# Rearranging VectorE's work at three places of a conditioned transformer block kernel in float32

## The chip, the cores and the metric

The kernel runs on one core of a Trainium2 chip. The metric is the device time of one execution in microseconds; times of several runs are given as their median.

In profiles PE is TensorE (its weight loads PEld), DVE VectorE, ACT ScalarE, POOL GpSimd and SP SyncE, which issues most DMAs.

## The reference

Two batch entries of 2048 rows with 512 columns go through one block; everything is float32.

```
emb  = silu(cond) @ ada_w + ada_b                     # per entry, six rows of 512
shift_msa, scale_msa, gate_msa, shift_mlp, scale_mlp, gate_mlp = split(emb, 6)
norm  = ln(x) * (1 + scale_msa) + shift_msa
h     = gelu(norm @ ssm_w1 + ssm_b1)                  # exact gelu, 512 -> 512
x     = x + gate_msa * (h @ ssm_w2 + ssm_b2)          # 512 -> 512
norm2 = ln(x) * (1 + scale_mlp) + shift_mlp
hf    = gelu_tanh(norm2 @ ff_w1 + ff_b1)              # 512 -> 1024
out   = x + gate_mlp * (hf @ ff_w2 + ff_b2)           # 1024 -> 512
```

## The kernel before, in words

The 4096 rows are cut into eight blocks `i` = 0 to 7 of 512 rows; blocks 0 to 3 are of the first batch entry, 4 to 7 of the second. A block passes through four products, which the tiles are named for: `hA` (ssm first), `oA` (ssm second, added to x), `hC` (ff first) and `oC` (ff second, added to x). In steady state the order on TensorE is `hC_i`, `oA_(i+1)`, `oC_i`, `hA_(i+2)`.

No product is computed plainly. `hA`, `oA`, and block 0's `hC` and `oC` use seven half-size products, P1, P2, P6, P5, P7, P3, P4 in this order, in place of eight. Sums of quarters of both operands are made ahead, and the results of several products are collected in three PSUM banks, `y` (P1, P6, P7, P4), `x` (P2) and `v` (P5, P3). `hC` of blocks 1 to 7 is a list of 26 products (`HK_P`, counted from 0 here) over registers: the quarters of norm2 and sixteen `forms`, which the 20 steps of `HK_B` make from them (line 819). `oC` of these blocks (`residual_in_leaves`) runs P1, P5, P6 and P7 as whole products and splits the other three once more into "leaves", seven small products `r` = 0 to 6 in the same order, with P7's matmuls spread between them.

The schedule is written by hand: every engine executes its instructions in the order in which the program issues them. `hook(hooks, places, ops)` spreads a list of operations over named places, and a place's operations are issued when its product and the reading of its bank have been issued (for `hC` the places are the product numbers). A place may hold work for any engine, so a hook fixes the place in that engine's queue alone. A PSUM bank that a later product adds to, or that a later tile takes over, is free only when the reading has ended: that is what TensorE can wait for.

What the diff touches:

- `hidden` makes a first product. Its `after` reads the banks: `take_first` (line 639 on VectorE, 637 on ScalarE) copies P1, P6 and P5 out with the bias added, lines 645, 652 and 655 add P2, P7 and P3 to these copies on VectorE, and ScalarE applies the gelu. `on_act` says who does `take_first`. It is used for block 0's `hC` (two groups of half the columns each) and for `hA`.
- `gb5_0` (line 1061) multiplies the ff bias row by the gate of the first entry and subtracts one half from the other, `apart_row`. `seed` later copies that row into the banks of `oC_0`.
- A gate is folded into the second weights once per batch entry. At the end of block 3's iteration `weight_of_second` gives eight multiplications of `fw2` by the gate (VectorE, line 395) and four sums of it (GpSimd, line 347), and `leaves_of_weight` four sums for the double leaves and four for the single ones (VectorE, line 347). Their list `fold` is spread over `First(5)`, that is `hA_5`, then `hC_4` and `oA_5`.
- A norm is `stats` (VectorE), `scales` (GpSimd), `normal` (ScalarE, line 539, or VectorE), `turn` (VectorE transposes of 32 by 32, line 550), `move` (16 DMAs, line 559, which put the blocks in place) and `moved` (modulation by scale and shift, line 582 on ScalarE, 584 on VectorE). Then come the sums or forms.
- In `oC_i` line 735 reads whole products, lines 773 and 776 the leaves. P7's bank is read in two steps behind leaf `r` = 4.
- For block 7 there is no `hA` between `oC_6` and `hC_7`. Its 20 forms, `late_forms`, are made on VectorE while `oC_6` ends and `hC_7` begins: seven in `oC_6`, thirteen at products 0 to 4.

Of the kernel before, what the change touches and what calls it, by code (L numbers as in the profile page):

```python
# [140 lines left out]
def kernel(  # L141
# [16 lines left out]
    nc = tc.nc  # L158
# [459 lines left out]
    def hidden(name, rhs, wops, bT, func, lo, hi, g, hooks, order=ORDER, on_act=False):  # L618
# [14 lines left out]
        def take_first(dst, src, r):  # L633
            if on_act:
                for j in range(2):
                    b = bT[:, r * half + m0 + j : r * half + m0 + j + 1]
                    nc.scalar.activation(dst[:, j], src[:, j], AF.Identity, bias=b)
            else:
                nc.vector.tensor_tensor(dst, src, bias(r), ALU.add)  # L639

        def after(p, ps, _):
            if p == "P1":
                take_first(s1, ps["y"], 0)
# [3 lines left out]
            elif p == "P6":  # L647
                take_first(u2, ps["y"], 0)
            elif p == "P5":
                take_first(s5, ps["v"], 1)  # L650
# [57 lines left out]
    def residual_in_leaves(name, i, hops, wops, leaf_wops, kdim, hooks, last=False):  # L708
# [58 lines left out]
        places = {1: "P5", 3: "P7", 4: "R4", 5: "P3", 6: "P4"}  # L767
        for r, f in enumerate(LEAVES):
# [8 lines left out]
            if r == 4:  # L777
                read("P7", "22", "21")
# [44 lines left out]
    class First:  # L823


        def __init__(self, i, rhs, hooks, order=ORDER, hA=None, on_act=False):
            if hA is None:
                hA = big_tile(f"hA_{i}")
            self.i, self.lo, self.hi = i, hA[:, : KD // 2, :], hA[:, KD // 2 :, :]
            hidden(f"hA_{i}", rhs, w1_ops, b1T, AF.Gelu, self.lo, self.hi, 0, hooks, order, on_act)  # L830
# [10 lines left out]
    class Second:  # L841
# [6 lines left out]
        def group(self, g, rhs, hooks):  # L848
            hidden(f"hC_{self.i}_{g}", rhs, fw1_ops, fb1T, AF.Gelu_apprx_tanh, self.lo, self.hi, g, hooks)
# [210 lines left out]
    def gb5_0():  # L1060
        nc.vector.tensor_tensor(gb[5], gate[5, 0], gb[5], ALU.mult)
        apart_row(gb[5], nc.gpsimd)
# [31 lines left out]
    hook(hooks, ("P7",), [gb5_0] + n2_sums[1:] + [lambda c=c: n1[2].normal(c) for c in range(C)])  # L1094
# [9 lines left out]
    hook(hooks, ("P2",), [n1[2].move])  # L1104
# [4 lines left out]
    hC.group(0, n2[0].ops, hooks)  # L1109
# [34 lines left out]
    hA[2] = First(2, n1[2].ops, hooks, on_act=True)  # L1144
# [14 lines left out]
    for i in range(1, NBLK):  # L1159
# [5 lines left out]
        if i == 1:  # L1165
            leaf_wops, leaf_fold = leaves_of_weight(fw2_sb, fw2_s, nc.gpsimd)
            hook(hooks, (5, 7, 9, 11, 13, 14, 15, 16), leaf_fold)
# [12 lines left out]
        if fold:  # L1180
            hook(hooks, (0, 0, 1, 1), fold[:4])
            hook(hooks, (5,), fold[4:8])
        hook(hooks, (0, 0, 0, 0, 1, 1, 1, 2, 2, 3, 3, 4, 4), late_forms)
# [13 lines left out]
        if nxt:  # L1197
# [3 lines left out]
            if fold:  # L1201
                hook(hooks, ("P1", "P2", "P6", "P5", "P5", "P7", "P7", "P3"), fold[8:])
# [7 lines left out]
        fold = None  # L1210
# [5 lines left out]
        if nxt:  # L1216
# [3 lines left out]
            turns = ("P2", "P2", "P6") if nx2 else ("P1",)  # L1220
# [12 lines left out]
        if nxt:  # L1233
            moved = n2[i + 1].moved((None,) if nx2 else (None, nc.vector))
            hook(hooks, ("P7",) if nx2 else ("P5", "P7", "P5", "P7"), moved)
# [7 lines left out]
        if nxt:  # L1243
            late = {}

            def form(eng):

                fb[i + 1] = n2[i + 1].registers()
                return sums_of_registers(HK_B, fb[i + 1], (eng,))

            if not nx2:

                def late_form(n):
                    if n == 0:
                        late["ops"] = form(nc.vector)
# [3 lines left out]
                hook(hooks, ("R4",) * 3 + ("P3",) * 2 + ("P4",) * 2, late_forms[:7])  # L1259
                late_forms = late_forms[7:]  # L1260

        residual_in_leaves(f"oC_{i}", i, hC, fw2_ops, leaf_wops, KH // 2, hooks, last)
# [4 lines left out]
        if nx2:  # L1267
            run(form(nc.gpsimd))

        if refold5:  # L1270
            take_gate(5, b)
            fw2_ops, fold = weight_of_second(fw2_sb, fw2_s, gate[5, b], (nc.vector,))
            leaf_wops, leaf_fold = leaves_of_weight(fw2_sb, fw2_s, nc.vector)
            fold += leaf_fold
        hooks = {}
        if refold5:
            hook(hooks, ("P6",), [multiply_5])
            hook(hooks, ("P5", "P7", "P3", "P4"), fold[:4])
            fold = fold[4:]
# [51 lines left out]
```

## The time and the profile before

| | us |
|---|---|
| median of 3 runs | 597.12 (597.0 to 598.76) |
| profiled execution | 597.23 |
| its span, first to last instruction | 595.4 |
| PE busy | 582.9 (98%) |
| DVE busy | 405.9 (68%) |
| POOL busy | 388.8 (65%) |
| ACT busy | 234.3 (39%) |
| mean granted TensorE clock | 0.998 |

A row of a timeline gives the start in us, the time in us (of several instructions from the first's start to the last's end), engine, line, operation, what it writes and reads, the shapes and the number of instructions; in brackets the idle time of the engine before it and what ended it. A row of waits names the engine that waited, its line, what it waited for, and the total, the number and the longest of the waits. A row of a stretch gives its bounds and length, the busy time and the number of instructions of each engine, the granted clock, and the share and rate of the DMAs.

### The profile page before, as it was taken

To read this page: it belongs to the slowest core of one execution; us is meant where nothing else is said; L and a number is where in the kernel's file an instruction comes from. 1 tells how busy PE (TensorE), PEld (TensorE's weight loads), DVE (VectorE), ACT (ScalarE), POOL (GpSimd) and SP (SyncE) were. 2 spreads that over 40 slices of the span, in tenths; PEclk is the share of its full clock that TensorE was granted. 3 is DMA by queue.
4 is the path that set the end of the run, shared out by engine and by line. 5 is a ranking of instruction groups with operands and counts; after the bars stand their busy time and mean duration, and the time that the engine had idled before them with its cause. 6 is when DMAs were issued, how large, how long until landed. Compare 5 with 4: busy or idle time off the path is not lost.

```text
span 595.4 us, 8969 instructions
## 1 busy us (share of the span) xinstructions
PE 582.9 (98%) x3127; PEld 512.5 (86%) x3127; DVE 405.9 (68%) x734; ACT 234.3 (39%) x396; POOL 388.8 (65%) x471
## 2 busy tenths in 40 slices
PE   7999999999999999999999999999999999998997
PEld 4888888888889888998889988888888988897886
DVE  4978898897566475675756778864756446559663
ACT  2235437405532374134811456134553236121420
POOL 1875439999991968539983699938687293800260
PEclk9999999999999999999999999999999999999999
DMA  8990332300324105440153602231030400031002
GB/s 317 395 381 13 81 72 78 101 36 35 69 75 120 41 0 116 141 134 2 31 129 72 212 1 55 87 72 71 1 72 1 142 2 1 1 72 70 2 0 72
DMA packets 24376, 50.17 MB, mean 84 GB/s; under 512 B 4576, under 2 KB 5644, under 8 KB 23436
## 3 DMA queue, kind: packets, MB, share of 16 engines
q1 hardware_dynamic: 20608, 44.86, 24.1%
q10 hardware_dynamic: 3724, 4.75, 3.3%
q8 instruction: 25, 0.41, 0.3%
q14 instruction: 19, 0.16, 0.1%
HBM read 26.51 MB, written 8.40 MB: 59 GB/s over the span
## 4 chain that ended last, share of the span: by engine, by line
PE 85%; DVE 4%; POOL 4%; DMA 2%; issue 2%; SPq 1%; ACT 1%; DVEq 0%; POOLq 0%
PE py_oC L724 11%; PE px_hC L881 9%; PE py_hA L465 9%; PE py_hC L881 7%; PE pv_hC L881 7%; PE py_oA L465 7%; PE pl_oC_P_y L757 6%; PE pv_hA L465 4%; PE pv_oA L465 3%; PE pv_oC L724 3%; PE pl_oC_P_v L757 3%; PE px_hA L465 2%; PE py_oC L465 2%; PE py_hC L465 2%; PE px_oA L465 2%
## 5 line engine op out<-in xcount | busy, mean ns | idle before, releaser
L582 ACT ACTIVATE nT<-nT,mod,mod 128x512 f32<-128x512 f32 x54 | 39.6, 802 | 103.5 <-DMA nT<-blocks 78.0
L539 ACT ACTIVATE nT<-x,nmr,rstd 128x512 f32<-128x512 f32 x56 | 42.4, 803 | 53.6 <-POOL nmr L526 38.8
L347 POOL TENSOR_TENSOR hSC<-hClo,hChi 128x512 f32<-128x512 f32 (+1 forms) x17 | 20.6, 1216 | 61.4 <-ACT hChi L876 47.6
L724 PE MATMUL py_oC<-fw,hClo 128*128 128x256 f32 x224 | 54.2, 380 | 1.2 <-DVE x L735 1.2
L508 POOL TENSOR_SCALAR ve<-mv 128x4 f32<-128x4 f32 x16 | 3.7, 231 | 77.0 <-DVE mv L500 70.2
L499 DVE BATCH_NORM_STATS2 st<-x 128x6 f32<-128x512 f32 x64 | 43.4, 678 | 5.2 <-DMA x<-in_x_dram 4.9
L724 PEld LDWEIGHTS py_oC<-fw,hClo 128*128 128x128 f32 x224 | 40.4, 190 | 5.7 <-DVE x L735 1.4
L881 PE MATMUL py_hC<-forms,fw 128*128 128x256 f32 x168 | 40.8, 379 | 0.0
L550 DVE STREAM_TRANSPOSE blocks<-nT 128x512 f32<-128x512 f32 x56 | 37.8, 694 | 3.8 <-ACT nT L539 3.5
L898 DVE TENSOR_TENSOR hClo<-hClo,py_hC 128x512 f32<-128x512 f32 x42 | 28.4, 680 | 16.6 <-ACT hClo L895 10.2
L819 POOL TENSOR_TENSOR forms<-forms 128x256 f32<-128x256 f32 x48 | 35.6, 742 | 2.8
L881 PEld LDWEIGHTS py_hC<-forms,fw 128*128 128x128 f32 x168 | 31.8, 190 | 4.4
L687 DVE TENSOR_TENSOR x<-py_oA,x 128x512 f32<-128x512 f32 x32 | 22.0, 688 | 19.5 <-PE py_oA L465 14.3
L898 DVE TENSOR_TENSOR hChi<-hChi,pv_hC 128x512 f32<-128x512 f32 x35 | 23.3, 683 | 14.7 <-PE pv_hC L881 14.7
L465 PE MATMUL py_hA<-nT,w 128*128 128x256 f32 x128 | 30.4, 381 | 0.0
L881 PE MATMUL px_hC<-forms,fw 128*128 128x256 f32 x112 | 27.8, 380 | 0.5 <-DVE forms L819 0.5
L876 ACT ACTIVATE hClo<-hClo,colsT 128x256 f32<-128x256 f32 x56 | 25.3, 499 | 6.7 <-DVE hClo L898 6.2
L465 PE MATMUL py_oA<-w,hA 128*128 128x256 f32 x112 | 26.5, 379 | 0.0
L465 PEld LDWEIGHTS py_hA<-nT,w 128*128 128x128 f32 x128 | 23.7, 190 | 3.1 <-DVE hA L639 0.2
L819 POOL TENSOR_TENSOR forms<-nT,forms 128x256 f32<-128x256 f32 x36 | 25.8, 739 | 0.5
L876 ACT ACTIVATE hChi<-hChi,colsT 128x256 f32<-128x256 f32 x56 | 25.1, 496 | 1.9 <-DVE hChi L898 1.9
L895 ACT ACTIVATE hClo<-px_hC 128x512 f32<-128x512 f32 x21 | 12.5, 597 | 33.7 <-PE px_hC L881 27.9
(290 smaller groups left out, 1583.9 us busy)
## 6 DMA issues: line engine op xcount, KB each, us to landing
nT<-blocks SPq DMA_DIRECT2D x168, 64.0 KB
x<-in_x_dram SPq DMA_DIRECT2D x7, 1024.0 KB
out_dram<-x SPq DMA_DIRECT2D x14, 512.0 KB
ada<-in_L_cond_ada_w_dram SPq DMA_DIRECT2D x6, 1024.0 KB
fw<-in_L_cond_ff_w_dram SPq DMA_DIRECT2D x2, 2048.0 KB
nT<-blocks ACTq DMA_DIRECT2D x56, 64.0 KB
w<-in_L_cond_ssm_w_dram SPq DMA_DIRECT2D x3, 1024.0 KB
fw<-in_L_cond_ff_w_dram SPq DMA_DIRECT2D x2, 1024.0 KB
```

The lines of the kernel that those rows point to most:

```text
L465: nc.tensor.matmul(ps[b][j * apart][:, j, :], lhs(p, j, k), rhs(p, j, k), start=(fresh and j * (not apart) == 0 and k == 0), stop=(p in (" ...
L499: nc.vector.bn_stats(st, xs[self.i][:, c, :])
L539: nc.scalar.activation(t, x_c, AF.Identity, bias=self.nmr[:, c : c + 1], scale=self.rstd[:, c : c + 1])
L550: nc.vector.transpose(self.bl[:, :, :, c, :].rearrange("p m k q -> p k m q"), self.nT[:, c, :].rearrange("p (k m q) -> p k m q", k=KD, m=C),)
L582: nc.scalar.activation(dst, src, AF.Identity, bias=shift, scale=scale)
L687: nc.vector.tensor_tensor(d, ps[BANK[p]][:, js], d, ALU.add)
L724: yield lambda j=j, k=k: nc.tensor.matmul(ps[BANK[p]][:, j, :], hops(p, j, k), wops[p][:, k, :], start=False, stop=(k == kdim - 1), skip_g ...
L757: nc.tensor.matmul(t[:, n, :], hops.leaves["P4" if which == "P4" else ("P2", "P3")[n]][f][:, k, :], leaf_wops["P4" if which == "P4" else ( ...
L819: eng.tensor_tensor(reg[d], reg[a], reg[b], ALU.add if f == "+" else ALU.subtract)
L876: nc.scalar.activation(h, h, AF.Gelu_apprx_tanh, bias=fb1T[:, m : m + 1])
L881: nc.tensor.matmul(ps[b][:, j, :], fa[ra][:, j * P : (j + 1) * P], fb[rb].rearrange("p a (c q) -> p c a q", q=Q), start=(fresh and j == 0) ...
L898: nc.vector.tensor_tensor(dest(d), dest(d), ps[b], op)
```

## The change

Three places are rearranged; no product is added or taken away.

- First group of block 0's `hC`: ScalarE does `take_first` for P6 and P5 (two instructions of 128x256 each) in place of VectorE. `gb5_0` moves from P7 of `oA_1` to P2 of this group, and its multiplication goes from VectorE to GpSimd, reading the gate's row in SBUF.
- Change of batch entry: six instead of four multiplications of `fw2` stand in `hA_5`, and two at product 0 of `hC_4` instead of four at products 0 and 1. The four sums for the single leaves move from `oA_5` to P1 and P5 of `oC_4` (its hook places "P1" and "P2"). In `oC_4` all four transposes of block 5's norm stand at "P6", behind the reading of P6, instead of at "P2", "P2", "P6", "P6".
- Before the last block: VectorE's two modulations stand behind leaf 2 instead of leaf 3 (new place "R2"). Eight late forms instead of seven are made in `oC_6`, and from an earlier place (behind leaf 3). Forms 0 to 11 are VectorE's, 12 to 19 GpSimd's. P7's bank is read behind leaf 6 instead of 4 in `oC_6`.

```diff
...
-    def hidden(name, rhs, wops, bT, func, lo, hi, g, hooks, order=ORDER, on_act=False):
+    def hidden(name, rhs, wops, bT, func, lo, hi, g, hooks, order=ORDER, on_act=()):
...
-        def take_first(dst, src, r):
-            if on_act:
+        def take_first(p, dst, src, r):
+            if p in on_act:
...
         def after(p, ps, _):
-                take_first(s1, ps["y"], 0)
+                take_first(p, s1, ps["y"], 0)
-                take_first(u2, ps["y"], 0)
+                take_first(p, u2, ps["y"], 0)
-                take_first(s5, ps["v"], 1)
+                take_first(p, s5, ps["v"], 1)
...
-    def residual_in_leaves(name, i, hops, wops, leaf_wops, kdim, hooks, last=False):
+    def residual_in_leaves(name, i, hops, wops, leaf_wops, kdim, hooks, last=False, read_p7=4):
...
-        places = {1: "P5", 3: "P7", 4: "R4", 5: "P3", 6: "P4"}
+        places = {1: "P5", 2: "R2", 3: "P7", 4: "R4", 5: "P3", 6: "P4"}
...
-            if r == 4:
+            if r == read_p7:
...
     class First:
-        def __init__(self, i, rhs, hooks, order=ORDER, hA=None, on_act=False):
+        def __init__(self, i, rhs, hooks, order=ORDER, hA=None, on_act=()):
...
-        def group(self, g, rhs, hooks):
-            hidden(f"hC_{self.i}_{g}", rhs, fw1_ops, fb1T, AF.Gelu_apprx_tanh, self.lo, self.hi, g, hooks)
+        def group(self, g, rhs, hooks, on_act=()):
+            hidden(f"hC_{self.i}_{g}", rhs, fw1_ops, fb1T, AF.Gelu_apprx_tanh, self.lo, self.hi, g, hooks, on_act=on_act)
         def products(self, fa, fb, hooks, act_first=False):
...
     def gb5_0():
-        nc.vector.tensor_tensor(gb[5], gate[5, 0], gb[5], ALU.mult)
+        nc.gpsimd.tensor_tensor(gb[5], gate_rows[5, 0], gb[5], ALU.mult)
...
-    hook(hooks, ("P7",), [gb5_0] + n2_sums[1:] + [lambda c=c: n1[2].normal(c) for c in range(C)])
+    hook(hooks, ("P7",), n2_sums[1:] + [lambda c=c: n1[2].normal(c) for c in range(C)])
...
-    hook(hooks, ("P2",), [n1[2].move])
+    hook(hooks, ("P2",), [n1[2].move, gb5_0])
-    hC.group(0, n2[0].ops, hooks)
+    hC.group(0, n2[0].ops, hooks, ("P6", "P5"))
...
-    hA[2] = First(2, n1[2].ops, hooks, on_act=True)
+    hA[2] = First(2, n1[2].ops, hooks, on_act=("P1", "P6", "P5"))
...
-            leaf_wops, leaf_fold = leaves_of_weight(fw2_sb, fw2_s, nc.gpsimd)
-            hook(hooks, (5, 7, 9, 11, 13, 14, 15, 16), leaf_fold)
+            leaf_wops, ops = leaves_of_weight(fw2_sb, fw2_s, nc.gpsimd)
+            hook(hooks, (5, 7, 9, 11, 13, 14, 15, 16), ops)
...
-            hook(hooks, (0, 0, 1, 1), fold[:4])
-            hook(hooks, (5,), fold[4:8])
-        hook(hooks, (0, 0, 0, 0, 1, 1, 1, 2, 2, 3, 3, 4, 4), late_forms)
+            hook(hooks, (0,), fold[:2])
+            hook(hooks, (5,), fold[2:6])
+        hook(hooks, (0, 0, 0, 1), late_forms)
...
-                hook(hooks, ("P1", "P2", "P6", "P5", "P5", "P7", "P7", "P3"), fold[8:])
+                hook(hooks, ("P1", "P2", "P6", "P5"), fold[6:10])
...
-        fold = None
+        leaf_fold, fold = fold and fold[10:], None
...
-            turns = ("P2", "P2", "P6") if nx2 else ("P1",)
+            turns = (("P6",) if leaf_fold else ("P2", "P2", "P6")) if nx2 else ("P1",)
+            if leaf_fold:
+                hook(hooks, ("P1", "P1", "P2", "P2"), leaf_fold)
...
-            hook(hooks, ("P7",) if nx2 else ("P5", "P7", "P5", "P7"), moved)
+            hook(hooks, ("P7",) if nx2 else ("P5", "R2", "P5", "R2"), moved)
...
-            def form(eng):
+            def form(engs):
-                return sums_of_registers(HK_B, fb[i + 1], (eng,))
+                return sums_of_registers(HK_B, fb[i + 1], engs)
                 def late_form(n):
-                        late["ops"] = form(nc.vector)
+                        late["ops"] = form((nc.vector,) * 12 + (nc.gpsimd,) * 8)
-                hook(hooks, ("R4",) * 3 + ("P3",) * 2 + ("P4",) * 2, late_forms[:7])
-                late_forms = late_forms[7:]
-
-        residual_in_leaves(f"oC_{i}", i, hC, fw2_ops, leaf_wops, KH // 2, hooks, last)
+                hook(hooks, ("P7",) * 4 + ("R4",) * 4, late_forms[:8])
+                late_forms = late_forms[8:]
+
+        residual_in_leaves(f"oC_{i}", i, hC, fw2_ops, leaf_wops, KH // 2, hooks, last, 4 if nx2 or last else 6)
-            run(form(nc.gpsimd))
+            run(form((nc.gpsimd,)))
-            leaf_wops, leaf_fold = leaves_of_weight(fw2_sb, fw2_s, nc.vector)
-            fold += leaf_fold
+            leaf_wops, ops = leaves_of_weight(fw2_sb, fw2_s, nc.vector)
+            fold += ops
-            hook(hooks, ("P5", "P7", "P3", "P4"), fold[:4])
-            fold = fold[4:]
+            hook(hooks, ("P5", "P5", "P7", "P3", "P4", "P4"), fold[:6])
+            fold = fold[6:]
```

## The prediction

> **What bounds the kernel.** I read the page's busy line first, then the waits of PE, then the stretches between like points of the schedule, then DVE's timeline inside the stretches that are too long.
>
> ```profile
> PE 582.9 (98%) x3127; PEld 512.5 (86%) x3127; DVE 405.9 (68%) x734; ACT 234.3 (39%) x396; POOL 388.8 (65%) x471
> ```
> PE is busy for 582.9 of 595.4 us, and no edit takes a matmul away. So the change can only win what PE stands idle, and the waits of PE (in total us, times, longest) name every place:
>
> ```profile
> PE px_hC L881 <- DVE hChi L898: 1.5, 1, 1.5
> PE py_oC L724 <- DVE x L735: 1.2, 1, 1.2
> PE py_hC L881 <- DVE forms L819: 0.9, 1, 0.9
> PE px_hC L881 <- DVE forms L819: 0.5, 1, 0.5
> PE py_hC L465 <- DVE hClo L639: 0.3, 1, 0.3
> ```
> All five wait for DVE. Short waits are hidden in merged rows, so I measure each place as a stretch against a like one (length first, then busy time of PE, PEld, DVE, ACT, POOL):
>
> ```profile
> 72.56:84.15 11.59, 11.21 (x49) 8.79 (x48) 11.42 (x23) 4.85 (x7) 3.73 (x4) 1.00 0.22 51
> 84.15:96.24 12.09, 12.09 (x58) 10.64 (x56) 9.23 (x17) 8.78 (x14) 10.48 (x18) 1.00 0.27 69
> 202.32:224.81 22.49, 22.49 (x105) 19.68 (x104) 15.34 (x24) 15.29 (x29) 17.19 (x19) 1.00 0.03 6
> 260.09:329.94 69.85, 69.85 (x366) 62.50 (x365) 45.55 (x85) 30.35 (x52) 51.91 (x64) 1.00 0.28 78
> 329.94:401.97 72.03, 70.66 (x366) 62.41 (x365) 55.28 (x97) 30.41 (x53) 58.36 (x64) 1.00 0.28 79
> 541.64:567.71 26.07, 23.22 (x107) 19.67 (x106) 20.07 (x42) 10.92 (x22) 5.01 (x4) 1.00 0.11 41
> ```
> - **A**, the first group of the first ff product: 84.15 to 96.24 holds seven products without a gap, 1.727 us each. 72.56 to 84.15 holds six, so 10.36 would do: 1.23 us lost.
> - **B**, the block in which the second batch entry's gate is folded in: 72.03 against 69.85, 2.16 us with rounding of the starts. By rows: 0.30 at 348 us (products), 0.30 at 375 (oA_5), 1.36 at 390 (oC_4).
> - **C**, the last ff products: 26.07 against 22.49, 3.58 us.
>
> Together 6.97 us, the most this change can bring in these places. The granted clock is 1.00 throughout, so it plays no part.
>
> **A: the first group.** DVE was busy 11.42 of 11.59 us here. PE's P6 needs P1's reading, P7 needs P6's, P3 needs P5's (one bank each).
>
> ```profile
> 73.91 0.68 DVE L639 TENSOR_TENSOR hClo<-py_hC,colsT 128x512 f32<-128x512 f32 x1
> 74.51 1.29 DVE L550 STREAM_TRANSPOSE blocks<-nT 128x512 f32<-128x512 f32 x2
> 77.52 0.65 DVE L639 TENSOR_TENSOR hClo<-py_hC,colsT 128x512 f32<-128x512 f32 x1
> 101.62 0.84 ACT L637 ACTIVATE hA<-py_hA,colsT 128x256 f32<-128x256 f32 x2 [0.27 <-PE py_hA L465]
> ```
> Moving gb5_0's product off DVE frees 0.60 (70.32 to 70.93): P1's reading begins at 73.3 instead of 73.9, ends at 74.0, and P6 can start at its due 74.29. P6's and P5's readings leave DVE (two steps of 0.60). ScalarE does one as a pair in 0.84 (row L637). At P6's end, 76.02, ScalarE is in L646: its table load ended at 76.16 and the gelu takes 0.63, so the pair ends near 77.6 and P7 is due at 77.75. The rows show Identity on both sides of a gelu without a table load of its own, so I add none. Queued behind this pair on ScalarE is P5's pair (due 77.95) and nothing else until L653. On DVE the next reading, P7's, falls at 79.8 and ends 80.4, before P4 is due at 81.26. On GpSimd gb5_0 now costs a 128x512 step (1.27) and the 0.73 it had before. It stands at P2, behind the nS sums, which therefore start 0.7 earlier; after it GpSimd sat idle for 8.8 us (75 to 85), so it is covered; without that cover it would delay n2's scales by 2.0. First reader of gb[5] is the seed at 104. Gain 1.23 less 0.08: **1.15**, bounds 0.6 (ScalarE late by 0.5) and 1.23. The later DVE and GpSimd work of this stretch hangs on PE and on these readings and shifts with it, so the gain is not handed back.
>
> **B: the second entry's folds and transposes.**
>
> ```profile
> 388.32 1.42 DVE L550 STREAM_TRANSPOSE blocks<-nT 128x512 f32<-128x512 f32 x2 [2.54 <-ACT nT L539]
> 389.67 0.65 DVE L735 TENSOR_TENSOR x<-py_oC,x 128x512 f32<-128x512 f32 x1
> ```
> DVE stood 2.54 us for ScalarE's normals, turned two, and only then read P6 of oC_4, ready at 387.9; PE's P7 matmul waited for that. With all turns at P6 the reading comes first: 1.36 goes. What is late next: the first leaf's readings now queue behind four turns; the normals end at 390.41, the last turn at 391.15, the readings at 391.8, and the leaf product P6 is due at about 391.6 once PE is 0.6 earlier: 0.25 stays. Two fw2 folds (0.60 each) go from the products into First(5): P5 takes two, P4 two. P7's reading there slips from 338.78 to 339.1 and P4 is not due before 340.31, so nothing. DVE then reaches the products 1.2 us sooner, and the 0.30 at 348 goes. The four single-leaf sums (4.4 us of DVE with GpSimd beside them, 373.3 to 379) leave oA_5, so its P7 reading is no longer behind them: 0.30 goes. They reappear behind P1 and P5 of oC_4: 2.2 us behind each, and DVE idles there 1.03 before P5's reading and 2.54 before the turns. PE's P6 ends near 387.1, the sums at 386.8: covered by 0.3. The DMAs of n2's move start at 391.2 against 391.55. Its modulated blocks end at 403.2, GpSimd could not start the forms before 406.9, so 3 us of cover remain when PE comes earlier. Gain **1.9**; bounds 1.0 (the sums at the slowest such row, 1.49 each) and 2.16.
>
> **C: the last forms.** Columns of the last three lines: count, then min/median/max ns.
>
> ```profile
> 539.37 1.28 DVE L735 TENSOR_TENSOR x<-py_oC,x 128x512 f32<-128x512 f32 x2
> 540.56 0.41 DVE L819 TENSOR_TENSOR forms<-nT 128x256 f32<-128x256 f32 x1
> 542.22 0.41 DVE L819 TENSOR_TENSOR forms<-forms 128x256 f32<-128x256 f32 x1
> L819 POOL TENSOR_TENSOR forms<-forms x48: 720/728/907, 122.0 to 484.6; 128x256 f32<-128x256 f32 x48
> L819 DVE TENSOR_TENSOR fw<-fw,fw_s x4: 832/881/942, 103.9 to 132.0; 128x256 f32<-128x256 f32 x4
> L819 DVE TENSOR_TENSOR forms<-forms x8: 414/420/425, 542.2 to 549.7; 128x256 f32<-128x256 f32 x8
> ```
> PE is free at 541.64 (541.19 and four leaf matmuls). Product 0 needs form 3 of the program (register 20, ended 542.6), product 3 needs form 10, product 8 a reading that came behind the late forms. After: DVE's two modulations run from the end of leaf P6's readings, 535.04, to 536.04 (ScalarE's of the same transfer started at 534.89, so it has landed), four forms at 537.25 to 538.8, leaf P7's readings to 539.55. Product 0's wait, 1.05, is gone. GpSimd's eight forms need register 21 and start at 538.6, early, because nothing stands before them in its queue. They run beside DVE's forms 4 to 7. DVE's adds with both inputs in SBUF take 0.42 alone and 0.83 to 0.94 beside GpSimd (100 to 132 us); the nearest rows are those, so 3.3 us for four: 542.85. Then four leaf readings (1.06) and P7's two (1.2), now last: 545.1. GpSimd has finished (five at 0.87, three at 0.69). Forms 8 to 10 depend on each other, 0.45 each: 546.45. Product 3, due at 544.23, starts at 546.6: 2.35 stays. Product 8 is then due at 550.9, and DVE's readings for it end near 550.2. The moved P7 readings keep no product 0 waiting: in the program of before its bank is that of leaf tile pl_oC_6_P4_x, read at r = 1; the seeded bank comes to product 6. Gain 3.58 - 2.35, about **1.2**. Bounds: no slowing at all, product 3 at 544.8, gain 3.0; the slowest such row, 1.38 each, loss 1.0.
>
> [...]
>
> **Sum.** 1.15 + 1.9 + 1.2 = 4.25. The profiled execution took 597.23 (span 595.4 and 1.8 around it), 0.11 over the median of 597.12: 597.12 - 4.25 = 592.9.
>
> **Rivals.**
> - *No contention in C*: GpSimd's steps fall where DVE reads PSUM. For it: the first add after a reading took 0.41 or 0.42 at 106.2, 116.0, 126.8 and 137.1. Against: the other rows. 6.05 off, 591.1.
> [...]
> - *It does not do what it says*: in A or B a next late reading takes the place of the old one, and with C at its slow end less than 1.8 is won: 595.4 to 598.
> - *Slower*: DVE's two modulations at R2 stand for the transposed blocks. Every reading and form of C is queued behind them on DVE. Costs 1 us per us once the landing is later than about 535.5; it pays back all 4.25 and 1.8 more from a landing of 541.5 on: 599 or more. For it: the same move in block 4 took 8.7 us from first issue to modulation, here 7.1. Against: 8.7 would mean 536.5, only 1 us lost.
>
> **How the numbers follow.** Forecast 0.59, no contention 0.13, port eats C 0.13, not as it says 0.09, slower 0.06. A measurement of this kernel tells about 0.3% (1.8 us) from no change; the first three are faster by more: 0.85. Range 590.6 (a little more than the no-contention case, the full 6.97 gives 590.2) to 595.3 (port at its slowest): it leaves out about 0.15.
>
> **What would show it.** Right: 72.56 to the second group shrinks to 10.4; the fold block to 70.1; no PE wait for L735; product 0 of the last block without a wait and one wait for L819 of about 2 us at product 3; DVE's forms there half at 0.42, half near 0.85. Wrong: PE waiting for ACT in the first group, for DMA behind R2, or L639/L735 still among PE's waits; GpSimd's forms starting only after product 1.

## The result, and the profile after

The changed kernel took 594.5 us (median of 6 runs, 592.64 to 595.09) against 597.17 for the kernel before (6 runs, 597.0 to 598.76). The ratio is 0.9948 [0.9931, 0.9964]: 0.5% faster. The forecast was 592.9, in a range of 590.6 to 595.3. The profiled execution took 592.64, with a span of 590.8; the forecast for that kind of execution was 592.98 (597.23 less 4.25). So the steps of the sum came out almost exactly, while the median lies 1.6 us higher. That difference is a story of its own, told with the first experiment.

The busy line of the page after:

```profile
PE 581.2 (98%) x3127; PEld 512.9 (87%) x3127; DVE 402.6 (68%) x723; ACT 236.0 (40%) x400; POOL 396.1 (67%) x480
```

And PE's waits (us in total, times, longest):

```profile
PE px_hC L881 <- DVE forms L819: 2.1, 1, 2.1
PE pada L274 <- DMA ada<-in_L_cond_ada_w_dram: 1.7, 2, 1.5
PE idle L970 <- POOL ident masks.py:199: 1.3, 1, 1.3
```

PE executes the same 3127 instructions. Its busy time fell from 582.9 to 581.2, because some short stalls stood as busy time before: in A 11.21 us, where the same products now take 10.36. In place of the five waits for DVE there is one, in front of product 3 of the last block; the other two lines are the start of the program. The stretches that the prediction measured, in the profile after (length first, then busy time of PE, PEld, DVE, ACT, POOL, then the granted clock):

```profile
72.48:82.84 10.36, 10.36 (x50) 9.04 (x49) 10.06 (x20) 6.86 (x12) 4.99 (x5) 1.00 0.19 44
328.63:398.59 69.96, 69.96 (x367) 62.42 (x365) 54.24 (x97) 29.48 (x52) 58.17 (x64) 1.00 0.28 79
538.25:563.04 24.79, 22.69 (x106) 19.69 (x105) 18.07 (x31) 10.92 (x22) 8.38 (x9) 1.00 0.11 43
```

- **A** went from 11.59 to 10.36: 1.23 gained, no gap left.
- **B** went from 72.03 to 69.96: 2.07 gained.
- **C** went from 26.07 to 24.79: 1.28 gained.

The sum is 4.58; the span fell from 595.4 to 590.8.

In A, ScalarE's row is the one on which the estimate turned. The pair for P6 ended at 77.43 (76.61 and 0.82) and P7 started at 77.66, on time:

```profile
74.78 1.28 ACT L646 ACT_TABLE_LOAD   x1
76.08 0.63 ACT L646 ACTIVATE hClo<-hClo 128x512 f32<-128x512 f32 x1
76.61 0.82 ACT L637 ACTIVATE hClo<-py_hC,colsT 128x256 f32<-128x256 f32 x2
77.86 0.84 ACT L637 ACTIVATE hChi<-pv_hC,colsT 128x256 f32<-128x256 f32 x2 [0.42 <-PE pv_hC L465]
```

In B, P6's reading now stands ahead of all four turns. It starts at 385.86, when PE has finished P6, and the turns wait for ScalarE behind it without holding anyone:

```profile
385.86 0.69 DVE L735 TENSOR_TENSOR x<-py_oC,x 128x512 f32<-128x512 f32 x1 [1.43 <-PE py_oC L724]
386.81 2.83 DVE L550 STREAM_TRANSPOSE blocks<-nT 128x512 f32<-128x512 f32 x4 [0.26 <-ACT nT L539]
```

In C, the timelines of PE, POOL and DVE around the one remaining wait:

```profile
543.11 1.10 PE L881 MATMUL px_hC<-forms,fw 128*128 128x256 f32 x4 [2.10 <-DVE forms L819]
535.21 1.77 POOL L819 TENSOR_TENSOR forms<-nT,forms 128x256 f32<-128x256 f32 x2 [15.42 <-DVE forms L819]
537.81 2.59 POOL L819 TENSOR_TENSOR forms<-forms 128x256 f32<-128x256 f32 x3
535.98 2.15 DVE L819 TENSOR_TENSOR forms<-nT,forms 128x256 f32<-128x256 f32 x3
538.05 0.94 DVE L819 TENSOR_TENSOR forms<-forms 128x256 f32<-128x256 f32 x1
539.98 1.27 DVE L735 TENSOR_TENSOR x<-py_oC,x 128x512 f32<-128x512 f32 x2
541.18 1.78 DVE L819 TENSOR_TENSOR forms<-forms 128x256 f32<-128x256 f32 x3
```

While POOL works on its forms, four of DVE's take 3.0 us (535.98 to 538.99); alone they took 0.41 or 0.42 each just before. The average hides the pattern: the first of the four took 0.41 and the other three 0.94 or 0.95 each. Taken one by one, the steps of the two engines (the last of the four is the row at 538.05 above):

```profile
535.99 0.99 POOL L819 TENSOR_TENSOR forms<-nT,forms 128x256 f32<-128x256 f32 x1
536.32 0.95 DVE L819 TENSOR_TENSOR forms<-nT,forms 128x256 f32<-128x256 f32 x1
536.94 0.90 POOL L819 TENSOR_TENSOR nT<-nT,forms 128x256 f32<-128x256 f32 x1
537.19 0.94 DVE L819 TENSOR_TENSOR forms<-nT,forms 128x256 f32<-128x256 f32 x1
537.81 0.90 POOL L819 TENSOR_TENSOR forms<-forms 128x256 f32<-128x256 f32 x1
```

Each of these DVE adds ends about 0.28 us after the end of the POOL step beside which it started, and each POOL step about 0.58 after the end of the DVE add before it: the two engines take turns, one pair in 0.87. Forms 8 to 10 stand behind P7's readings and end at 542.96. Product 3 was due at 540.84 and starts at 543.11: 2.27 lost, of which 2.10 shows as a wait.

### The profile page after: what moved, and what is told of

Its sections match the earlier page's. It is cut to its first block, busy times and chain, and to the rows that moved or that the text cites. A ratio compares the mean times of both kernels' runs of the same rounds, so it can differ in the third digit from the quotient of the medians.

```text
span 590.8 us, 8982 instructions
## 1 busy us (share of the span) xinstructions
PE 581.2 (98%) x3127; PEld 512.9 (87%) x3127; DVE 402.6 (68%) x723; ACT 236.0 (40%) x400; POOL 396.1 (67%) x480
## 4 chain that ended last, share of the span: by engine, by line
PE 95%; DVE 2%; DMA 2%; SPq 0%; issue 0%
PE py_oC L724 12%; PE px_hC L881 10%; PE py_hA L465 9%; PE py_oA L465 9%; PE py_hC L881 8%; PE pv_hC L881 8%; PE pl_oC_P_y L757 6%; PE pv_hA L465 5%; PE pv_oA L465 5%; PE pv_oC L724 4%; PE pl_oC_P_v L757 3%; PE px_hA L465 2%; PE py_oC L465 2%; PE py_hC L465 2%; PE px_oA L465 2%; DMA ada<-in_L_cond_ada_w_dram 2%
## 5 line engine op out<-in xcount | busy, mean ns | idle before, releaser
L898 DVE TENSOR_TENSOR hClo<-hClo,py_hC 128x512 f32<-128x512 f32 x42 | 28.5, 681 | 17.3 <-ACT hClo L895 9.6
L819 POOL TENSOR_TENSOR forms<-forms 128x256 f32<-128x256 f32 x51 | 38.1, 748 | 3.0
L819 POOL TENSOR_TENSOR forms<-nT,forms 128x256 f32<-128x256 f32 x38 | 27.7, 749 | 15.9 <-DVE forms L819 15.4
L898 DVE TENSOR_TENSOR hChi<-hChi,pv_hC 128x512 f32<-128x512 f32 x35 | 23.3, 683 | 14.3 <-PE pv_hC L881 14.3
```

The source lines that it names most:

```text
L819: eng.tensor_tensor(reg[d], reg[a], reg[b], ALU.add if f == "+" else ALU.subtract)
L898: nc.vector.tensor_tensor(dest(d), dest(d), ps[b], op)
```

## The experiments

Theory at the outset: the three places work as forecast, and what separates the median (594.5) from the profiled execution (592.64) is TensorE's clock. Five of the six executions of the changed kernel had a mean granted clock of 0.996 or 0.997 and spans of 592.4 to 593.2; the profiled one had 1.000.

**The changed kernel once more**, unchanged, for a trace of a longer execution.

> The changed kernel once more, unchanged. Its profiled execution took 592.64 (span 590.8, clock 1.000), its five other runs 594.3 to 595.1 (spans 592.4 to 593.2, clock 0.996 to 0.997), a gap of 1.9 us that no edit explains. Theory 1 (the end): the products take what they took in the profile, and the last stores after the last matmul take 4.6 us in some executions and 6 to 7 in others, so a longer tail at the low clock that TensorE has when idle gives both the longer span and the lower mean clock. Theory 2 (the middle): the 2.1 us wait of PE at product 3 of the last ff products lets the clock fall to half for some 4 us in most executions, which costs 2 us there. Both expect a median of about 594.5; in a profile of a long execution theory 1 shows full clock and 0.216 us per matmul of 256 columns up to the last matmul, theory 2 shows slow matmuls behind the wait.

Measured: 593.86 us (6 runs, 592.78 to 595.34), ratio 0.9935 [0.9918, 0.9952]. Three executions had a clock of 0.996 or 0.997 and took 594.46 to 595.34, three had 0.999 or 1.000 and took 592.78 to 593.26. The profiled one was of the longer kind. Its stretches (the granted clock is the third number from the end):

```profile
541.00:544.00 3.00, 0.98 (x5) 0.53 (x3) 2.93 (x7) 1.03 (x2) 1.74 (x3) 1.00 0.75 298
544.80:548.20 3.40, 3.40 (x9) 2.68 (x8) 2.04 (x4) 0.60 (x1) 0.00 (x0) 0.50 0.00 0
548.30:556.00 7.70, 7.70 (x38) 6.77 (x37) 4.13 (x6) 2.56 (x5) 0.00 (x0) 1.00 0.00 0
```

Its PE timeline behind the wait:

```profile
544.09 1.34 PE L881 MATMUL px_hC<-forms,fw 128*128 128x256 f32 x4 [2.10 <-DVE forms L819]
545.21 1.91 PE L881 MATMUL py_hC<-forms,fw 128*128 128x256 f32 x4
546.92 1.68 PE L881 MATMUL px_hC<-nT,fw_s 128*128 128x256 f32 x4
548.44 1.03 PE L881 MATMUL py_hC<-forms,fw 128*128 128x256 f32 x4
```

The wait is the same 2.10, but 0.7 us after it ends TensorE runs at half clock for 3.41 us, and four matmuls take 1.91 where they take 1.03. That costs half of 3.41, 1.7 us, which is the distance between the two groups of times. (This execution is another 0.8 longer because its start waited longer for DMAs: the second conditioning product started at 12.66 instead of 11.82.) The rival, that the time is lost at the end of the program, falls too: from the last matmul to the end it is 4.4 us in this trace and in the shorter one, and the clock falls there in the traces of the shorter executions as well (at 590.5 in the changed kernel's, at 586.8 in that of the kernel with GpSimd held back, below).

The traces show how long such a stretch is. The record of full clock lasts 587.09 us in the trace of the kernel before (from 6.2 us into the span) and 583.68 in the changed kernel's (from 6.9): 172 and 171 times 3.4133, and 3.413 apart. In the traces with half clock before the end of the products, this one and four from below, one stretch at half clock lasts 3.4 and two in a row 6.8, and from there to the next fall it is 44.4 us in four and 576.9 in one, 13 and 169 times 3.413. So the record of these seven traces is made in stretches of 3.413 us, and their phase differs from execution to execution; where a trace has one fall alone, the stretches are counted back from it. This lets one read from each profile how long TensorE stood idle in one stretch, and what clock it had in the next. Idle is time in which none of the profile's matmuls runs. The table has the places of the profiles with the longest idle times; the later rows come from the experiments below.

| place and wait (us) | idle in one stretch (us) | next stretch |
|---|---|---|
| kernel before, start and product waits | 1.53 at most | full |
| changed kernel, start, 0.20 and 1.53 | 1.53 | full |
| no ScalarE, product 3, 2.11, split by a boundary | 1.14 and 0.97 | full |
| turns back, oC_4, 1.71 | 1.62 | full |
| changed kernel, product 3, 2.10, split | 1.75 and 0.35 | full |
| five steps, start, 0.79 and 1.53, split | 1.83 | full |
| eight steps, start, 0.94 and 1.53, split | 1.86 | full |
| no ScalarE, start, 0.77 and 1.54 | 1.92 | half |
| changed kernel again, product 3, 2.10 | 2.10 | half |
| turns back, product 3, 2.11 | 2.11 | half |
| five steps, product 3, 2.59 | 2.59 | half |
| eight steps, product 3, 5.40 | 3.41 | half |
| the same wait, its rest in that half-clock stretch | 1.69 | half |
| end of the program, changed kernel and all forms on VectorE | 0.74 and 1.04 | full |
| end of the program, four profiles | 2.04 to 2.97 | half |

After a stretch at full clock, the clock stayed with up to 1.86 idle and fell from 1.92 on. After a stretch at half clock less was enough, 1.69 in the one case here. An estimate from these figures, with all phases taken as equally likely: a wait of 2.10 lies in one stretch with at least 1.86 (1.92) of itself for a share (3.413 + 2.10 - 2 x 1.86) / 3.413 = 0.53 (0.49) of the phases. Over all batches 15 of 68 executions of the kernel before were longer too (598.48 to 599.26); it has no such wait late, so these are put down to the start, of which more below. With this share added, the sum is 60 to 63% longer executions; over both batches the changed kernel had 8 of 12. The sum is rough, since the share of the kernel before differs between batches, from 2 of 23 to 4 of 9.

**C undone**, A and B kept:

```
-hook(hooks, (0, 0, 0, 1), late_forms)
+hook(hooks, (0, 0, 0, 0, 1, 1, 1, 2, 2, 3, 3, 4, 4), late_forms)
-... else ("P5", "R2", "P5", "R2"), moved)
+... else ("P5", "P7", "P5", "P7"), moved)
-late["ops"] = form((nc.vector,) * 12 + (nc.gpsimd,) * 8)
+late["ops"] = form((nc.vector,))
-hook(hooks, ("P7",) * 4 + ("R4",) * 4, late_forms[:8])
+hook(hooks, ("R4",) * 3 + ("P3",) * 2 + ("P4",) * 2, late_forms[:7])
...
```

> The change without its part C (the late forms, the modulations and the reading of P7 before the last block are as before). Theory: A and B are independent of C and give 1.23 and 2.07 us, so span 595.4 - 3.3 = 592.1 and PE's waits of before in the last block return (forms L819 0.9 and 0.5, hChi L898 1.5). Rival (the three parts share one slack): part of A and B is lost again at the end and the span is above 593. On the clock: if the long wait of part C caused the lower clock (theory 2 of e1), this kernel's runs stand 1.8 above their span with the clock of before, 0.998, and are about as fast as the changed kernel; if it is the end of the execution, their clock scatters between 0.996 and 1.000 as the changed kernel's does.

Measured: span 592.1, 3.3 less than before and 1.3 more than with C. Median 594.16 (7 runs, 594.06 to 596.0), ratio 0.9955 [0.9939, 0.9971]. PE's waits for DVE are the old three of the last block:

```profile
PE px_hC L881 <- DVE hChi L898: 1.5, 1, 1.5
PE py_hC L881 <- DVE forms L819: 0.9, 1, 0.9
PE px_hC L881 <- DVE forms L819: 0.5, 1, 0.5
```

So A and B are worth 3.3 and C 1.3 in the span. But the median of the twelve executions with C is 594.4, no better than 594.16 without it: C turns three short waits into one of 2.1, and an execution whose clock falls there loses 1.7. Without C three of seven were longer, with it 8 of 12, which puts the one median among the short executions and the other among the long. By the means (594.9 without C, 594.1 with it) some of the gain stays.

**All twenty late forms on VectorE**, the rest of C kept:

```
-late["ops"] = form((nc.vector,) * 12 + (nc.gpsimd,) * 8)
+late["ops"] = form((nc.vector,))
```

> The changed kernel with all twenty late forms on VectorE, at the same places: GpSimd stands still while they are made. Theory (contention): forms 4 to 7 take 0.42 each instead of 0.94, product 3 of the last block waits about 0.5 us instead of 2.1; but forms 12 to 19 now stand before VectorE's readings behind product 1, so about 1.5 us of wait returns near products 7 and 8. Sum about 2.0 to 2.4 of wait, time within 0.5 us of the changed kernel. Rival (queue only, no contention): forms 4 to 7 take as long as in the changed kernel, product 3 still waits 2 us, and with the wait at products 7 and 8 on top the time is 1.5 us longer.

Measured: 593.82 us (6 runs, 592.97 to 595.96), ratio 0.9938 [0.9919, 0.9957], span 591.1. PE's waits for DVE:

```profile
PE px_hC L881 <- DVE hChi L898: 1.3, 1, 1.3
PE px_hC L881 <- DVE forms L819: 0.3, 1, 0.3
```

DVE's forms 4 to 7 in its timeline:

```profile
536.18 1.09 DVE L819 TENSOR_TENSOR forms<-nT,forms 128x256 f32<-128x256 f32 x3
537.19 0.42 DVE L819 TENSOR_TENSOR forms<-forms 128x256 f32<-128x256 f32 x1
```

The four forms end 1.43 us after they start instead of 3.0, and product 3 waits 0.3: the slowing was GpSimd's doing, as the prediction had it. It isn't a way out, because DVE's readings of the product banks then come late (1.3 at L898) and the span stays within 0.3 of the changed kernel's. Three of the six executions were longer ones (594.59 to 595.96, the last at a clock of 0.992), though the profile shows no wait above 1.3 behind the start; what lowered their clock wasn't profiled.

**GpSimd held back.** Eleven of VectorE's forms before P7's readings, and a 128x4 operation on GpSimd that reads form 10, so that its own forms start behind it:

```
-hook(hooks, (0, 0, 0, 1), late_forms)
+hook(hooks, (1,), late_forms)
...
+if n == 12:
+    held = small.tile([P, C], F32, tag="held", name="held", bufs=1)
+    nc.gpsimd.tensor_scalar(held, forms[:, 5, 0, :C], 1.0, None, ALU.mult)
 late["ops"][n]()
...
-hook(hooks, ("P7",) * 4 + ("R4",) * 4, late_forms[:8])
-late_forms = late_forms[8:]
+hook(hooks, ("P7",) * 4 + ("R4",) * 7, late_forms[:11])
+late_forms = late_forms[11:]
```

> The changed kernel with two edits in part C: forms 4 to 10 all stand behind leaf 4 (before the last leaves' and P7's readings), and GpSimd's first form is held until form 10 is made, by a 128x4 step that reads it. Theory: without GpSimd beside them the seven forms take 0.38 apart, form 10 ends near 538.8 (in the changed kernel's times, 542.9 there), product 3 (due 540.8) and product 8 (due 545.2) find all they need, PE has no wait in the last block: span 590.8 - 2.2 = 588.6. Rival (queue only): GpSimd's steps do not matter, the seven forms take 0.7 each, form 10 ends near 541 and product 3 still waits about 0.3.

Measured: 590.69 us (4 runs, 590.67 to 591.95), ratio 0.9887 [0.9871, 0.9903], span 588.8. PE has no wait left after the start. DVE's forms 4 to 10 and POOL's first step behind them:

```profile
536.07 1.08 DVE L819 TENSOR_TENSOR forms<-nT,forms 128x256 f32<-128x256 f32 x3
537.08 1.80 DVE L819 TENSOR_TENSOR forms<-forms 128x256 f32<-128x256 f32 x4
538.96 0.23 POOL L1260 TENSOR_SCALAR held<-forms 128x4 f32<-128x4 f32 x1 [19.08 <-DVE forms L819]
```

The seven forms take 2.8 us and end 2 us before product 3 needs the last. GpSimd starts 4.2 us later than in the changed kernel and still is in time for every product. The two engines' forms were never needed at the same time.

**The turns back**, in the changed kernel:

```
-turns = (("P6",) if leaf_fold else ("P2", "P2", "P6")) if nx2 else ("P1",)
+turns = ("P2", "P2", "P6") if nx2 else ("P1",)
```

> The changed kernel with one edit taken back: in the block in which the second entry's gate is folded in, the turns of n2's blocks stand again two behind P2 and two behind P6, so that two of them are ahead of P6's reading. Theory (the turns ahead of the reading held PE): DVE stands at the first turn for ScalarE's normals, P6's reading comes two turns later, and a wait of PE for L735 comes back in oC_4, 1.2 to 1.6 us. Two pairs of leaf sums now also stand in front of these turns. Span 592.1 to 592.5 (590.8 plus 1.3 to 1.7), hA_5 to hA_6 71.3 to 71.6 long. Rival (the sums that left oA_5 and the folds made all of block 4's gain): no wait for L735, 69.96 long, span 590.8.

Measured: 596.52 us (12 runs, 594.78 to 598.12), ratio 0.9988 [0.9976, 1.0]. PE's waits for DVE:

```profile
PE px_hC L881 <- DVE forms L819: 2.1, 1, 2.1
PE py_oC L724 <- DVE x L735: 1.7, 1, 1.7
```

Its DVE at the turns:

```profile
387.13 1.42 DVE L550 STREAM_TRANSPOSE blocks<-nT 128x512 f32<-128x512 f32 x2 [2.38 <-ACT nT L539]
388.47 0.65 DVE L735 TENSOR_TENSOR x<-py_oC,x 128x512 f32<-128x512 f32 x1
```

The stretch from hA_5 to hA_6 is 71.83 (328.94 to 400.77), 1.87 longer than in the changed kernel and a little over what was expected. The order of the turns carries most of B, now that the leaf sums stand in front of them. The twelve times lie in three groups: two at 594.8, six at 596.3 to 596.6 and four at 597.8 to 598.1 with a clock of 0.994. The last is about what two half-clock stretches would cost at 1.7 each (an estimate); where the second lay in those four wasn't profiled.

**P6's and P5's readings back on VectorE**, in the changed kernel:

```
-hC.group(0, n2[0].ops, hooks, ("P6", "P5"))
+hC.group(0, n2[0].ops, hooks)
```

> The changed kernel with one edit taken back: P6's and P5's readings of hC_0's first group go to VectorE again; gb5_0's product stays on GpSimd. Theory: moving the product alone frees 0.60 us ahead of P1's reading and two more steps of 0.60 come back later, so P6 starts on time, P7's reading on VectorE comes 1.2 us later than its 79.66, and P4, due at 81.11, waits for it 0.4 to 0.6 us. The stretch from 72.5 to the second group is 10.8 to 11.0 long, the span 591.2 to 591.4. Rival (ScalarE's two readings carry nearly all of the gain): 11.4 or more, span 591.8 or more. Rival (they carry nothing): 10.36, span 590.8.

Measured: 595.03 us (4 runs, 594.7 to 595.75), ratio 0.996 [0.9948, 0.9973]. The stretch of six products is 11.20 long, between the theory's 10.8 to 11.0 and the first rival's 11.4: of A's 1.23 the move of gb5_0's product brings 0.39 and ScalarE's two readings 0.84.

```profile
74.19:85.39 11.20, 11.11 (x49) 8.79 (x48) 11.03 (x22) 4.85 (x7) 5.03 (x5) 1.00 0.19 42
```

The PE timeline of the start, in the same profile:

```profile
9.22 1.08 PE L274 MATMUL pada<-ada,silu 128*32 128x128 f32 x32 [0.77 <-DMA ada<-in_L_cond_ada_w_dram]
11.84 1.59 PE L274 MATMUL pada<-ada,silu 128*32 128x128 f32 x32 [1.54 <-DMA ada<-in_L_cond_ada_w_dram]
13.37 3.07 PE L568 MATMUL pt<-ident,blocks 128*128 128x128 f32 x16
```

This profile also caught the other place where the clock falls. Two waits for DMA at the start, 0.77 and 1.54, put 1.92 us of idle time into one stretch, and the sixteen transposes behind them take 3.07 instead of 1.97. Product 3 waited 2.11 in the same execution without any harm, because a boundary cut its wait into 1.14 and 0.97. All four executions of this kernel were longer ones, at a clock of 0.996 or 0.997.

**A wait of a chosen length.** In the kernel with GpSimd held back, form 10's register is multiplied in place by 1.0 on GpSimd five, eight or four times, so that product 3 stands for the last of them:

```
-held = small.tile([P, C], F32, tag="held", name="held", bufs=1)
-nc.gpsimd.tensor_scalar(held, forms[:, 5, 0, :C], 1.0, None, ALU.mult)
+for _ in range(4):   # 7 in the run with eight, 3 in the run with four
+    nc.gpsimd.tensor_scalar(forms[:, 5], forms[:, 5], 1.0, None, ALU.mult)
+nc.gpsimd.tensor_scalar(forms[:, 5], forms[:, 5], 1.0, None, ALU.mult)
```

> The kernel of the held run, in which GpSimd first multiplies form 10's register by 1.0 in place five times before its own forms, so that product 3 stands for the last of them: a pure wait of TensorE in front of product 3. The multiplications start at 538.96; one of them costs between 0.35 (a little over the 0.23 of a 128x4 step) and 0.73 (a two-operand step of the same shape), so the wait is 0 to 1.9 us; most likely about 0.7 to 1.9. Theory (the wait in front of product 3 lets the granted clock fall in some executions, more often the longer it is): with a wait of 0.7 to 1.2 us, low-clock executions (1.2 to 1.7 us above the fast ones) in a quarter or fewer; with 1.2 to 1.9 about half. Rival (low-clock executions come from the start or the end and have nothing to do with this wait): one in four, as in the held run, whatever the wait is. Profiled span 588.8 plus the wait.

> As the run with five multiplications, with eight: a wait of 1.0 to 4.0 us in front of product 3, most likely 2.5 to 4. Theory: nearly every execution has the lower clock (at least three in four), and in a long execution's trace TensorE's matmuls behind the wait are twice as long for 3.4 us; the time is that of the held run plus the wait plus 1.7. Rival: one execution in four has the lower clock, the time is that of the held run plus the wait alone. Profiled span 588.8 plus the wait, or 1.7 more if the profiled execution is one with the lower clock.

> As the run with five multiplications, with four: one took 0.92 us there, so the wait in front of product 3 is 1.67 us here (2.59 less 0.92). Theory (the clock record goes in stretches of 3.413 us whose phase differs from execution to execution; the next stretch is at half clock when about 1.8 us of one are idle: 1.92 and more did it in the profiled runs so far, 1.75 and less did not): 1.67 us can't fill a stretch that far, so this wait never lowers the clock; executions are at 590.7 plus 1.67, 592.3 to 592.5, but for the one in six or seven that lose 1.3 to 1.9 us at the start, as the kernel before does too (6 of its 41). Rival (the chance grows evenly with the wait): with 0.75 at 2.1 and 2.6 us, about half of the executions low here, 593.6 to 594.1. Profiled span 588.8 plus 1.67, 590.5.

Measured, PE's wait for the last multiplication with five:

```profile
PE px_hC L881 <- POOL forms L1261: 2.6, 1, 2.6
```

And with eight:

```profile
PE px_hC L881 <- POOL forms L1261: 5.4, 1, 5.4
```

| steps | wait (us) | median, runs | ratio | longer executions |
|---|---|---|---|---|
| four | 1.65 | 592.72 (592.37 to 594.48), 6 | 0.9922 [0.9905, 0.994] | 2 of 6 |
| five | 2.59 | 594.76 (593.51 to 595.19), 5 | 0.9952 [0.9941, 0.9964] | 4 of 5 |
| eight | 5.40 | 599.0 (597.46 to 599.18), 11 | 1.0021 [1.0012, 1.003] | 11 of 11 |

One multiplication took 0.85 to 0.87, and one started every 0.93 to 0.95, above the 0.73 given as the most, so the waits with five and eight came out longer than expected. Four short executions of the first row are at 592.37 to 592.92, the held kernel's 590.7 and the wait. The one short execution with five is at 593.51, again the held kernel's time and the wait. With eight every execution is longer, by 6.8 to 8.5 us for 5.4 us of wait. By the same estimate from the table's limits a wait of 2.59 lowers the clock in 0.63 to 0.67 of the phases, 0.71 to 0.74 with the start's share (4 of 5 did), and one of 1.65 in none, which leaves the start's share with four steps (2 of 6). The even growth would give about three of six there, so these six runs don't settle it by themselves; the table of stretches speaks for a limit between 1.86 and 1.92.

**The held kernel once more.**

> The held run again, unchanged, for its share of low-clock executions. Theory: TensorE has no wait after the start, so only the start can lower the clock: about one execution in six or seven at 592 to 592.5, the others at 590.6 to 590.8; median 590.7. Rival (the one low execution of four was the rule, or some other place lowers the clock): a quarter to a half of the executions at 592 or more.

Measured: 592.09 us (5 runs, 590.76 to 592.18), ratio 0.9898 [0.9882, 0.9913]. Three of five had a clock of 0.995 or 0.996 and took 592.09 to 592.18; that is more than the theory gave, so the rival's share was nearer. Over both batches it is 4 of 9, median 591.67. No wait of TensorE is left after the start in its profile, so the start was the suspect.

**The start filled**: two, then one warm-up product more between the first and the second conditioning product, in the held kernel.

```
 modulation(0, 0)
+for _ in range(2):   # in the second run once, without the loop
+    nc.tensor.matmul(
+        idle, ident, ident.unsqueeze(1).to_broadcast([P, C, P]), start=True, stop=True
+    )
```

> The held kernel with two more of the warm-up matmuls of line 970 at the start, between the first and the second conditioning product, where TensorE waits 1.5 us for a DMA (0.57 us each at full clock, so 0.4 of the wait stays). Theory (the low-clock executions of the held kernel, 4 of 9, come from the start, where the waits of 0.3 to 0.8 and of 1.5 us can fall into one stretch of 3.413 us): no stretch of the start can be idle for 1.8 us now, so nearly every execution is at 590.6 to 590.9. Rival (they come from another place, or the start's stretch lowers the clock in another way): about four in nine at 591.7 to 592.2 as before. Second rival: the two matmuls delay the second conditioning product, 0.2 to 1 us more in every execution.

> The held kernel with one more warm-up product of line 970 instead of two between the first and the second conditioning product. It takes 0.99 us (the two took 1.98), so it fits into the 1.53 of the wait and delays nothing: 0.5 stays. Theory: no stretch of the start is idle for 1.8 us, so no execution has the lower clock, and with no delay the executions are at 590.6 to 590.9; where n2's last transposed blocks land late, as they did in the run with two, 591.7, still at a clock of 0.998 or more. Rival (the clock falls at another place): some of them, about four in nine, at 592 with a clock of 0.996.

Measured with two: 591.8 us (4 runs, 591.67 to 591.89), ratio 0.9907 [0.989, 0.9923]. With one: 591.64 us (5 runs, 591.05 to 591.7), ratio 0.9894 [0.9877, 0.9911]. No execution of the nine had a clock below 0.998, against 4 of 9 without the filling. By that the start was the held kernel's place, as far as nine executions can say. The time is not lower for it, though: the median of the nine is 591.67, as it is for the held kernel. Two products took 1.98 us, not the 1.1 assumed, and delayed the start by 0.3. And in both profiles DVE's modulations stood for the last transposed blocks, which had landed in time in both profiles of the held kernel (there they start at 531.84 and 531.95 without a wait). The rows are of the run with one: PE at the start, DVE at the modulations, PE in the products.

```profile
10.21 1.12 PE L997 MATMUL idle<-ident 128*128 128x512 f32 x2
11.82 1.08 PE L274 MATMUL pada<-ada,silu 128*32 128x128 f32 x32 [0.48 <-DMA ada<-in_L_cond_ada_w_dram]
533.42 1.00 DVE L584 TENSOR_SCALAR nT<-nT,mod,mod 128x512 f32<-128x512 f32 x2 [1.75 <-DMA nT<-blocks]
543.77 1.10 PE L881 MATMUL px_hC<-nT,fw_s 128*128 128x256 f32 x4 [0.86 <-DVE nT L819]
```

This is the mechanism of the prediction's slower rival, at a small price: a landing at least 1.6 us later costs 0.86 at a product. Why the last packets come late in these two programs wasn't found. One execution of the held kernel without the filling, 591.67 at a clock of 0.999, took as long; whether its packets were late too wasn't profiled.

## Why the prediction was right, and what it left out

**A** was forecast at 1.15 of 1.23; all 1.23 came. ScalarE was 0.2 us ahead of P7 where the working had 0.15, the 0.08 kept for lateness wasn't needed, and taking ScalarE's part away cost 0.84.

**B** was forecast at 1.9; 2.07 came. The turns carried most of it, as the run with the turns back shows: 1.87, more than the 1.36 of the working. The leaf sums now stand in front of them, which may be the reason; it wasn't tested apart. The 0.25 that the working left at the leaf product shrank to about 0.1: the block is 69.96 long, against 69.85 for the block without folds in the profile before.

**C** was forecast at 1.2; 1.28 came. Product 3 started 2.27 us late where 2.35 was worked out. The chain of reasons held too: forms 4 to 7 took 3.0 us beside GpSimd against the 3.3 estimated, and 1.43 with GpSimd kept off. That the size came out so close is partly luck. The working had GpSimd done before form 8, at 0.45 for each of forms 8 to 10, 1.35 in all. In the profile GpSimd's last step still ran, form 8 took 0.87, and the three took 1.78; this 0.43 was made up by the 0.3 of forms 4 to 7 and by their start, 0.2 earlier than worked out.

The adds took 0.95 at the most. In the rows DVE and GpSimd take turns, each step ending a fixed time after the other's, 0.28 and 0.58 us, where the steps take 0.42 and 0.73 alone; a pair took 0.87. No run shows a port, which the chances and the upper end of the range name; what the runs showed in its place is these turns, with forms 4 to 7 at 3.0 and 1.28 won in C. The rival without contention was right for one add of the four, the first behind a reading (0.41), and fell with the other three. The rival of modulations that stand for a DMA didn't come about in this change, but its mechanism is real, as the last two runs show: 0.86 at a product in each of the two.

**What the prediction left out** is one sentence of its first part: the granted clock is 1.00 throughout, so it plays no part. That was a reading of one execution of the kernel before, whose late waits are 1.48 at most. The change puts one wait of 2.1 in the place of five, and this one is long enough for the clock to fall in somewhat more than half of the executions, at 1.7 each. So the forecast of 592.9 describes the executions that keep the clock (592.64 to 593.26 were measured for these); the median is one of those that don't. Taking the profiled execution's difference for the difference of medians was the step that failed, by 1.6 us. That 594.5 still lies in the range is luck: the upper end, 595.3, was set for slower adds of VectorE's in C, and the median lies where C would have won nothing or lost up to 1.0 (594.1 to 595.1), while C's 1.28 came and the clock took 1.7.

It also left out the better order: forecasting that GpSimd's early start would double DVE's steps, the working could have asked who needs GpSimd's forms at 535. In the run with four steps they started with product 3 itself, and no product waited for one; holding them back is worth 2.0 us of span.

## What to carry to other kernels

Removing waits of TensorE by gathering them into one can lose what it gains, if the one that is left is long enough for the clock to fall (here C won 1.3 of span, and a fall behind the wait of 2.1 that it left cost 1.7); count what a wait costs behind it, over several executions, not in one profile. When two engines slow each other on the way to a deadline, ask which of them has the deadline, and hold the other with a dependence rather than giving the work back (here holding GpSimd won 2.0 us of span). A trace with clock 1.00 says nothing about executions in which the same idle time falls differently into the clock's stretches: of two traces of the changed kernel with the same wait of 2.10, one kept full clock (1.75 and 0.35 in two stretches) and one fell to half (2.10 in one).

## What the runs showed of the hardware that was not expected

- Half clock came in whole stretches of 3.413 us, fixed in phase within an execution and not between executions, after a full-clock stretch with 1.92 us of idle time or more, and not after one with 1.86 or less. A wait of 5.40 brought two such stretches in a row, the second after 1.69 us of idle time in a stretch that was itself at half clock.
- A one-input 128x256 step on GpSimd (multiplication by a constant, in place) took 0.85 to 0.87 us, more than the 0.73 of its two-input additions of the same shape.
- VectorE's two-input adds, 0.42 alone, took 0.94 or 0.95 beside GpSimd's, and GpSimd's 0.90 to 0.99 beside them against 0.73 alone. The two took turns: an add ended about 0.28 after the GpSimd step that it stood beside, the next GpSimd step about 0.58 after the add.
